# A two-layer attention megakernel: sums and deviations spread by way of DRAM, projection by adding transfers, the first image's keys first

## The chip, the cores and the metric

The kernel runs on one core of a Trainium2 chip. The metric is the device time of one execution in microseconds (us). Before the change it is 3413.48 us, the median of three runs between 3412.46 and 3414.23.

## The reference

The input is eight images of 256 channels and 32 × 32 positions, in fp32. Two layers follow each other.

```python
# layer 0, per image: group norm, then attention over a pooled pyramid
q  = einsum('bchw,oc->bohw', x, q_w)            # 1024 queries, 8 heads of 32
kv = einsum('bchw,oc->bohw', x, kv_w)
# k and v maps: pooled to 32x32, 16x16, 11x11, 5x5 -> 1426 tokens;
# each level p becomes p + depthwise3x3(p) + bias; then layer norm over channels
attn = softmax(q_g @ k.T * 32**-0.5); out_att = attn @ v
# a small channel attention of the heads (w_attn) and the projection follow
x = x + proj(...)

# layer 1, per image: 1024 tokens of 256 channels
t = t + attn1(layernorm(t))      # one head of 256
t = t + moe(layernorm(t))        # 8 experts of three 256x256 layers, softmax gates
```

The gates of the experts depend on the mean over all eight images, so that they are known only when layer 1's attention of the last image has ended.

## The kernel before, in words

Everything lies as channels on the 128 partitions (two halves, `c` or `k`) by positions in the free dimension. All work in fp32.

**The spine.** `attention` (line 880) runs 384 steps in order: 8 images × 2 halves of the channels (4 heads each) × 2 halves of the queries × 12 chunks of 128 keys. A step makes scores (`scores`, line 1458: four matmuls of 32 rows into the `sc` bank), one exponential of 128 × 2048 on ScalarE into one of six `pt` buffers (line 1465), and, a step later, the product with the values (`values`, line 1468). Every second step an adding transfer from the POOL queue adds one `pt` to the one before it (`add`, line 1480). After 12 steps the unit's sum of exponentials is formed: VectorE adds the pairs (line 1494), four matmuls add over the partitions (line 1499), so that each of the four heads' 512 sums stands 32 times, once on each of its partitions, in `rec` (128 × 512). `normalise` (line 1506) takes the reciprocal of all 128 × 512 and multiplies the unit's output `att` by it. ScalarE adds up sums and reciprocals for a check of their bounds. There are 32 such units.

**The background.** All other work of layers 0 and 1 lies in Python generators ("threads"), which yield what they need next (an engine and tiles). The class `Flow` (line 656) keeps a model of each engine's time while the program is being written, with a cost for every instruction (`cost`, line 711) and a lag until its result is there. For a transfer the lag is 3.0 us from the SP queue and `LANDING` = 9.5 us from POOL (line 784). After each step `Flow.step` (line 849) lets those threads go on whose inputs are, by this model, near enough; `NEAR` and `AHEAD` (lines 35 and 36) say how near for each engine. `finish` (line 862) drives threads until a condition holds. The order on every engine is fixed by this, and on the chip each engine, and each engine's transfer queue, goes through it in order.

**The first image.** Nothing can hide its preparation: `prepare` (line 1337) normalises the image, `first_maps` (line 1128) makes its key and value maps, values first (m = 2, 3) and keys (m = 0, 1) after, and then the queries. The large level's 3 × 3 taps of the keys run on TensorE as diagonal matmuls (`first_keys`, line 1179, with diagonals from `first_diagonals`, line 1116), those of the values and all small levels on VectorE (`first_taps`, line 1217). `by_tokens` (line 1254) turns them into normalised tokens. The spine starts when two of three groups of keys are there (line 1803). The diagonals (line 1119), the second value map's `p` (line 1136), and the two key maps' `p` and `acc` (lines 1139 and 1141) lie in buffers of the `pt` ring until used. For later images the taps all run on VectorE (`convolve`, line 1229).

**The projection.** When an image's four units are done, `project` (line 1514) makes four matmul pairs of 128 × 512. For each it loads a quarter of the image's x into the only `xr` buffer (line 1525), VectorE adds product, bias and x there (line 1533), and the sum is stored to `t1` in DRAM (line 1535). The last image goes through one big buffer.

**Layer 1.** `layer1` (line 1577) loads `t1`, and `scale_tokens` (line 1540) divides each token by its deviation: transposes to tokens (line 1550), statistics on VectorE, a power on POOL, and then the row of 128 × tiles deviations must be spread over all partitions. For that POOL multiplies the identity by the deviations (`diag`, line 1560), and a matmul with ones puts them on every partition (line 1568); VectorE multiplies by what stands in PSUM (line 1573). This happens once per image for 1024 tokens (two pieces of 512) and once for each 256 tokens of layer 1's output (`norm`, line 1679).

**The experts** (`experts`, line 1979) take over TensorE when the spine has ended, while the last image's layer 1 still runs in the background. Until the gates are known, `first` (line 2117) makes an expert's first layer as 8 products of 256 columns; later, `first7` (line 2213) makes it as 7.

Of the kernel before, what the change touches and what calls it, by code (L numbers as in the profile page):

```python
# [11 lines left out]
ALU = mybir.AluOpType  # L12
# [4 lines left out]
P = 128  # L17
# [18 lines left out]
NEAR = {"DVE": 1.5, "ACT": 2.0, "POOL": 1.0, "SP": 10.0}  # L36
BUFS = {"sm": 2, "sx": 1}
PACE2 = 8.0
LANDING = 9.5
# [616 lines left out]
class Flow:  # L656
# [90 lines left out]
    def note(self, engine, op, ins, args, kwargs):  # L747
# [35 lines left out]
        if "dma" in op:  # L783
            lag = 3.0 if engine == "SP" else LANDING
# [95 lines left out]
def attention(tc, kit, f, outer, ended, nb, consts, x, t1, t2, hn, bounds, vecs, q_t, kv_t, proj_t, gqk_t, wqk, wqkv, vecs1, w1_d, w1c, gate_d, wrc, vecs2, bnvec):  # L880
# [6 lines left out]
    with ExitStack() as ctx:  # L887
# [38 lines left out]
        pjw = weight(proj_t, "v", 256, l1)  # L926
# [27 lines left out]
        def mix():  # L954
# [66 lines left out]
            bdt = T(l1, [P, 2, P], "diag4")  # L1021
# [40 lines left out]
        def pool(*tiles):  # L1062
            return "POOL", tiles, None

# [49 lines left out]
        first, large, whole, pooled = {}, [], [], []  # L1114

        def first_diagonals():

            middle = T(l1, [P, 2, P], "rec1")
            rest = T(work, [P, 4, 512], "pt", bufs=6).rearrange("p a (b q) -> p (a b) q", q=P)
# [8 lines left out]
        def first_maps(xp):  # L1128


            for m in (2, 3, 0, 1):
                c = m % 2
                if m == 2:
                    p, acc = pmap, T(work, [P, NK], "acc", bufs=3)
                elif m == 3:
                    p = T(work, [P, 4, 512], "pt", bufs=6).rearrange("p j q -> p (j q)")
                    acc = T(work, [P, NK], "acc", bufs=3)
                else:
                    both = T(work, [P, 4, 512], "pt", bufs=6).rearrange("p j q -> p (j q)")
                    p = both  # L1140
                    acc = T(work, [P, 4, 512], "pt", bufs=6).rearrange("p j q -> p (j q)")
                for t in (p, acc):
                    if t is not pmap:
                        f.split(t, 512, HW)
                first[m] = p, acc
            for s0, w in KEY_SLICES:
                if s0 >= HW:
                    yield until(lambda: pooled)
                for m in (2, 3, 0, 1):
                    c = m % 2  # L1150
                    p, acc = first[m]
                    src = source(xp, s0, w)
                    yield pe(src, tag="sm")
                    ps = small()
                    for k in range(2):
                        f.pe.matmul(
                            ps[:, :w],
                            lhsT=kvw[:, k, m * P : (m + 1) * P],
                            rhs=src[:, k, :],
                            start=k == 0,  # L1160
                            stop=k == 1,
                        )
                    f.act.activation(p[:, s0 : s0 + w], ps[:, :w], AF.Copy)
                    for s, n in enumerate(SIDES):
                        a, z = max(OFFS[s], s0), min(OFFS[s] + n * n, s0 + w)
                        if a < z and (m >= 2 or s):
                            f.act.activation(
                                acc[:, a:z],
                                ps[:, a - s0 : z - s0],
                                AF.Identity,  # L1170
                                bias=db(c, s),
                                scale=mid[:, c * 4 + s : c * 4 + s + 1],
                            )
                if s0 == 512:
                    large.append("maps")
                    f.spawn(first_keys(), 5)
            whole.append("maps")

        def first_keys():
# [3 lines left out]
            for half in range(2):  # L1183
                for m in range(2):
                    p, acc = first[m]
                    pin = p[:, : n * n].rearrange("p (h w) -> p h w", h=n)
                    yield pe(p[:, : n * n], middle, rest, tag="sm")
                    ps = small()
                    pout = ps.rearrange("p (h w) -> p h w", w=n)
                    for i, tap in enumerate((4, 0, 1, 2, 3, 5, 6, 7, 8)):  # L1190
                        dy, dx, y0, y1, x0, x1 = windows(tap, n)
                        y0, y1 = max(y0, 16 * half), min(y1, 16 * half + 16)
                        f.pe.matmul(
                            pout[:, y0 - 16 * half : y1 - 16 * half, x0:x1],
                            lhsT=rest[:, 8 * m + i - 1, :] if i else middle[:, m, :],
                            rhs=pin[:, y0 + dy : y1 + dy, x0 + dx : x1 + dx],
                            start=i == 0,
                            stop=i == 8,
                        )
                    f.act.activation(acc[:, half * 512 : half * 512 + 512], ps, AF.Identity, bias=db(m, 0))  # L1200
                large.append(("keys", half))
# [135 lines left out]
        def prepare(b):  # L1337

            xi = xs.pop(b) if b in xs else load_x(b)
# [1125 lines left out]
```

## Time and profile before

| | us | share of the span |
|---|---|---|
| span of the profiled execution | 3418.4 | |
| TensorE matmul busy (PE) | 3204.7 | 94% |
| TensorE weight load busy (PEld) | 1781.8 | 52% |
| VectorE busy (DVE) | 2285.8 | 67% |
| ScalarE busy (ACT) | 1675.6 | 49% |
| GpSimd busy (POOL) | 499.0 | 15% |

A row of the groups says: line, engine, operation, output <- inputs, shapes, count, busy time and mean in nanoseconds, and then the idle time before these instructions with what ended it. All recorded operations go through one helper, so that all carry line 669; the tiles' names tell them apart. An fp32 matmul of the program is two records in the profile. A row of the waits says who waited for whom: us in total, times, the longest. In the table of transfers the numbers are KB of each and us from issue to landing.

### The profile page before, as it was taken

What the parts mean: (1) busy time and instruction counts of PE and PEld (TensorE: products, weight loads), DVE (VectorE), ACT (ScalarE), POOL (GpSimd) and SP (SyncE); (2) the same over time, 40 slices, a digit from 0 to 9 for tenths busy, and PEclk for the clock granted to TensorE, in tenths of its full rate; (3) what the DMA queues carried; (4) which work ended last, traced back from release to release, by engine and by line L of the source; (5) the groups of instructions that cost most, each with busy time, mean ns of one, the idle gap of its engine ahead of it and who ended that gap; (6) DMA issues with size and microseconds to landing.
All of it is one profiled execution on the core that took longest, in us unless ns stands there. A gap on an engine that the chain in (4) does not pass through costs nothing.

```text
span 3418.4 us, 39922 instructions
## 1 busy us (share of the span) xinstructions
PE 3204.7 (94%) x15264; PEld 1781.8 (52%) x15264; DVE 2285.8 (67%) x3914; ACT 1675.6 (49%) x2193; POOL 499.0 (15%) x616
## 2 busy tenths in 40 slices
PE   7588899999999899999999989998999999999998
PEld 3232244444444334434434356646777777777776
DVE  6587798888888878888644543216776666666665
ACT  3466667566676576566664523342223333333332
POOL 3122213122141221321211200004000000000000
PEclk9699999999999999999999999999999999999999
DMA  1257565555555655555665663123440000000000
GB/s 48 63 114 165 135 135 115 125 126 123 138 116 122 161 108 128 127 122 129 148 134 132 141 191 124 56 77 132 140 160 31 19 29 27 19 19 19 19 13 20
DMA packets 105032, 337.47 MB, mean 99 GB/s; under 512 B 12976, under 2 KB 38328, under 8 KB 81600
## 3 DMA queue, kind: packets, MB, share of 16 engines
q0 software_dynamic: 24576, 172.51, 25.8%
q1 hardware_dynamic: 76896, 160.35, 13.6%
q8 instruction: 122, 2.00, 0.2%
q10 hardware_dynamic: 3360, 1.97, 0.2%
q14 instruction: 78, 0.64, 0.1%
HBM read 98.33 MB, written 63.97 MB: 47 GB/s over the span
## 4 chain that ended last, share of the span: by engine, by line
PE 74%; DMA 5%; ACT 4%; DVE 2%; issue 2%; POOL 1%; SPq 0%; ACTq 0%; DVEq 0%; POOLq 0%
PE bank L669 25%; PE sm L669 18%; PE y L669 11%; PE sc L669 8%; PE sx L669 6%; PE pv L669 6%; ACT pt L669 3%; DMA pt<-pt 2%; DMA t<-xr 1%; DMA xr<-in_x_dram 1%; DVE acc L669 0%; DMA hn<-hn 0%; DVE pt L669 0%; DVE rec L669 0%; DVE xr L669 0%
## 5 line engine op out<-in xcount | busy, mean ns | idle before, releaser
L669 ACT ACTIVATE pt<-sc 128x2048 f32<-128x2048 f32 (+1 forms) x384 | 720.7, 1877 | 317.1 <-PE sc L669 244.7
L669 PE MATMUL sc<-q,kn 32*128 32x512 f32 (+1 forms) x3072 | 452.4, 659 | 115.5 <-ACT pt L669 114.0
L669 DVE SCALAR_TENSOR_TENSOR acc<-p,vec,acc 128x225 f32<-128x225 f32 (+7 forms) x928 | 528.5, 576 | 35.7 <-ACT acc L669 11.2
L669 PE MATMUL bank<-h,w2e 128*128 128x512 f32 x1024 | 480.5, 595 | 0.0
L669 ACT ACTIVATE h<-bank,bnvec 128x512 f32<-128x512 f32 x302 | 233.1, 772 | 484.5 <-PE bank L669 464.4
L669 DVE TENSOR_TENSOR pt<-pt,pt 128x1024 f32<-128x1024 f32 x320 | 390.0, 1261 | 84.8 <-DMA pt<-pt 82.6
L669 PE MATMUL pv<-pt,vt 128*32 128x512 f32 (+1 forms) x3072 | 422.6, 623 | 0.0
L669 ACT ACTIVATE h<-c,bnvec 128x512 f32<-128x512 f32 x210 | 159.6, 807 | 318.6 <-DVE c L669 318.6
L669 POOL DMA_DIRECT2D pt<-pt x192 | 169.8, 884 | 923.2 <-ACT pt L669 788.8
L669 DVE TENSOR_TENSOR c<-p1c,bank 128x512 f32<-128x512 f32 x105 | 72.2, 688 | 314.9 <-PE bank L669 314.9
L669 PEld LDWEIGHTS sc<-q,kn 32*128 32x128 f32 (+1 forms) x3072 | 117.8, 181 | 311.5 <-ACT pt L669 209.4
L669 PEld LDWEIGHTS bank<-h,w2e 128*128 128x128 f32 x1024 | 194.8, 191 | 153.0 <-issue 141.4
L669 PEld LDWEIGHTS pv<-pt,vt 128*32 128x32 f32 (+1 forms) x3072 | 61.0, 109 | 306.6 <-issue 291.4
L669 POOL TENSOR_TENSOR rstd<-rstd,mhalf 128x4 f32<-128x4 f32 (+2 forms) x88 | 107.0, 1216 | 733.8 <-DVE rstd L669 593.7
L669 DVE TENSOR_TENSOR h<-h,gates 128x1024 f32<-128x1024 f32 x128 | 156.9, 1226 | 71.3 <-DMA h<-h 64.2
L669 PE MATMUL bank<-hn,w1e 128*128 128x256 f32 (+1 forms) x604 | 192.7, 448 | 10.1 <-DMA hn<-hn 10.1
L669 PE MATMUL y<-t,s3e 128*128 128x256 f32 x768 | 187.1, 380 | 0.0
L669 PE MATMUL sm<-p,v 128*128 128x256 f32 x736 | 173.8, 388 | 6.1 <-DVE xr L669 6.1
L669 ACT ACTIVATE p<-sm 128x512 f32<-128x512 f32 (+1 forms) x154 | 89.9, 584 | 173.7 <-PE sm L669 134.2
L669 PE MATMUL sm<-y,t 128*128 128x256 f32 x712 | 169.4, 385 | 2.1 <-ACT p L669 2.1
L669 PEld LDWEIGHTS bank<-hn,w1e 128*128 128x128 f32 x604 | 114.7, 191 | 99.9 <-issue 92.4
L669 PEld LDWEIGHTS sm<-p,v 128*128 128x128 f32 x736 | 139.3, 193 | 49.7 <-issue 24.4
(294 smaller groups left out, 4624.9 us busy)
## 6 DMA issues: line engine op xcount, KB each, us to landing
pt<-pt POOLq DMA_DIRECT2D x160, 1024.0 KB, 7.3
h<-h SPq DMA_DIRECT2D x80, 512.0 KB, 3.4
xi<-in_x_dram SPq DMA_DIRECT2D x16, 512.0 KB, 5.0
t<-t SPq DMA_DIRECT2D x8, 1024.0 KB, 6.9
res<-t SPq DMA_DIRECT2D x32, 256.0 KB, 4.4
t<-res SPq DMA_DIRECT2D x32, 256.0 KB, 2.6
hn<-res SPq DMA_DIRECT2D x32, 256.0 KB, 3.4
hn<-hn SPq DMA_DIRECT2D x16, 512.0 KB, 5.8
```

The lines of the kernel that those rows point to most:

```text
L669: ins = fn(*args, **kwargs)
```

## The change

It has four parts.

- **Reciprocals once each.** The 4 × 512 different sums of a unit are regathered by a transfer from `rec` into a 128 × 16 tile `few`, VectorE takes the reciprocal of those, they are stored as a 4 × 512 row in DRAM, and four transfers spread each head's row over its 32 partitions of `rec`. The check's sum is taken over `few`.
- **Layer 1's deviations by the same way.** In `scale_tokens` the deviations go to a row in DRAM and come back on all partitions, in place of diagonals on POOL, matmuls with ones, and a PSUM bank. So that the store is contiguous, a transpose now takes every eighth (or second) token.
- **Projection by adding transfers.** x is copied into `t1` from DRAM to DRAM when the image is prepared. ScalarE adds the bias and writes the product to `xr`, and a POOL-queue transfer adds it onto `t1`. The last image is left as it was.
- **First image's keys first.** The large level's keys are mapped first, its queries are a thread of their own, the spine starts with one group of keys, and the buffers are placed elsewhere: diagonals in layer 1's `t`, key accumulators in `kn` and `v`, the second value map in `acc`; only the key maps' `p` stay in the `pt` ring. In turn the fifth step must wait for all taps of the keys.

The model of the transfers is made finer (a lag that grows with the size), and SP transfers are issued only when their input is within 1 us of being there.

```diff
-NEAR = {"DVE": 1.5, "ACT": 2.0, "POOL": 1.0, "SP": 10.0}
+NEAR = {"DVE": 1.5, "ACT": 2.0, "POOL": 1.0, "SP": 1.0}
...
-            lag = 3.0 if engine == "SP" else LANDING
+            size = 4e-3 * out.shape[0] * out.free_size() if out.space != DRAM else 4e-3 * srcs[0].shape[0] * srcs[0].free_size()
+            lag = 2.0 + 0.0045 * size if engine == "SP" else 1.5 + 0.0078 * size
...
-            rest = T(work, [P, 4, 512], "pt", bufs=6).rearrange("p a (b q) -> p (a b) q", q=P)
+            rest = T(l1, [P, 16, P], "t")
...
-            for m in (2, 3, 0, 1):
...
+            for m in range(4):
+                if m < 2:
                     p = T(work, [P, 4, 512], "pt", bufs=6).rearrange("p j q -> p (j q)")
+                    acc = T(l1, [P, NK], "v") if m else T(work, [P, NK], "kn", bufs=3)
+                else:
+                    p = T(work, [P, NK], "acc", bufs=3) if m == 3 else pmap
                     acc = T(work, [P, NK], "acc", bufs=3)
...
+            for m, s0 in [(m, s0) for g in (0, 2) for s0 in (0, 512) for m in (g, g + 1)] + [(m, HW) for m in range(4)]:
...
+                    f.spawn(first_keys(0), 1)
+                    f.spawn(first_keys(1), 5)
...
+            if b < nb - 1:
+                f.sp.dma_start(t1[b], x[b].rearrange("(k p) n -> p k n", p=P))
...
+                f.spawn(queries(b, xi), 3)
                 yield from first_maps(xp)
...
-            return rec
+            few = T(work, [P, 16], "few")
+            yield sp(rec)
+            f.sp.dma_start(few, rec[::DH, :].rearrange("j (i k) -> j i k", k=16))
+            return rec, few
...
-            f.ve.reciprocal(rec, rec)
+            yield ve(few)
+            f.ve.reciprocal(few, few)
+            yield sp(few)
+            f.sp.dma_start(rows[n].rearrange("j (i k) -> (j i) k", k=16), few)
+            yield sp(rows[n])
+            for j in range(4):
+                f.sp.dma_start(rec[DH * j : DH * j + DH, :], rows[n][j : j + 1, :].to_broadcast([DH, 512]))
+            yield act(few)
+            f.act.activation(few, few, AF.Copy, accum_out=lo[:, column[n] : column[n] + 1])
+            yield ve(rec)
             f.ve.tensor_tensor(att, att, rec, ALU.mult)
...
-                        xt = T(work, [P, 512], "xr")
-                        f.sp.dma_start(xt, x[b, m * P : (m + 1) * P, sl])
...
+                        yield act(ps)
+                        f.act.activation(xt, ps, AF.Identity, bias=bias[:, m : m + 1])
+                        yield pool(xt)
+                        f.pool.dma_start(out=t1[b][:, m, sl], in_=xt, accum_op=ALU.add)
...
-                        f.pe.transpose(ps[:, o : o + P], src[:, c, (g + u) * P : (g + u + 1) * P], ident)
+                        f.pe.transpose(ps[:, o : o + P], src[:, c, g + u :: tiles], ident)
...
-                diag = T(l1, [P, m, P], f"diag{m}")
...
-                    rb[:, : m * P], lhsT=kit.ones, rhs=diag.rearrange("p t q -> p (t q)"), start=True, stop=True
...
+            f.sp.dma_start(row.rearrange("o (p u) -> (o p) u", u=tiles), r)
+            yield sp(row)
+            w = min(512, n)
+            for o in range(0, n, w):
+                rb = T(l1, [P, w], f"rb{w}")
+                f.sp.dma_start(rb, row[:, o : o + w].to_broadcast([P, w]))
                 yield ve(rb)
-                f.ve.tensor_tensor(d, d, rb[:, None, : m * P].to_broadcast([P, 2, m * P]), ALU.mult)
+                f.ve.tensor_tensor(d, d, rb[:, None, :].to_broadcast([P, 2, w]), ALU.mult)
...
-        f.finish(lambda: key_parts[0] > 1)
+        f.finish(lambda: key_parts[0] > 0)
...
+                if i == 4:
+                    f.finish(lambda: {0, 1}.issubset(whole))
```

## The prediction

> **What bounds the kernel now.** I read the page from the top: spans first, then busy time by engine, then the slices.
>
> ```profile
> span 3418.4 us, 39922 instructions
> PE 3204.7 (94%) x15264; PEld 1781.8 (52%) x15264; DVE 2285.8 (67%) x3914; ACT 1675.6 (49%) x2193; POOL 499.0 (15%) x616
> ...
> PE   7588899999999899999999989998999999999998
> ...
> DVE  6587798888888878888644543216776666666665
> ...
> PEclk9699999999999999999999999999999999999999
> ```
>
> TensorE is busy 94% of the span and idle 213 us. So time leaves in two ways: less TensorE work, or fewer of these 213 us. The low digits stand in the first slices. The table of stretches puts numbers on them (columns: length, then busy time of PE, PEld, DVE, ACT, POOL, then granted clock, DMA share, GB/s):
>
> ```profile
> 0.00:102.00 102.00, 68.56 (x191) 34.88 (x192) 70.33 (x161) 39.10 (x82) 35.43 (x57) 0.91 0.13 40
> 102.00:190.00 88.00, 62.46 (x319) 27.60 (x317) 46.09 (x121) 42.07 (x50) 10.51 (x9) 0.78 0.34 73
> 190.00:500.00 310.00, 262.49 (x1526) 94.80 (x1523) 256.91 (x448) 207.91 (x239) 67.20 (x78) 0.95 0.63 138
> 500.00:2000.00 1500.00, 1429.80 (x8119) 659.62 (x8118) 1132.10 (x1953) 928.95 (x1107) 332.38 (x389) 0.98 0.58 129
> ...
> 2350.00:3418.00 1068.00, 1054.39 (x4052) 769.42 (x4050) 675.27 (x1050) 345.56 (x539) 7.29 (x14) 0.99 0.14 47
> ```
>
> TensorE idles 33 us before 102 us, 26 to 190, 48 to 500, then 70 in 1500 us, and 14 in the last 1068. In the last stretch the experts run at TensorE's pace, and the change doesn't touch them. What TensorE waits for between 110 and 2030 us, from the waits:
>
> ```profile
> PE sc L669 <- ACT pt L669: 114.0, 95, 7.1
> PE sm L669 <- DVE xr L669: 12.3, 3, 6.1
> PE bank L669 <- DMA hn<-hn: 10.1, 1, 10.1
> ```
>
> The scores wait for the exponential ahead to empty their bank. Why that is late at the start, the timeline shows:
>
> ```profile
> 89.15 1.95 PE L669 MATMUL sx<-con,kt 128*128 128x128 f32 x4 [12.54 <-ACT kt L669]
> ...
> 102.46 2.09 PE L669 MATMUL sc<-q,kn 32*128 32x512 f32 x8
> ...
> 128.35 1.88 ACT L669 ACTIVATE pt<-sc 128x2048 f32<-128x2048 f32 x1 [6.43 <-DMA pt<-pt]
> ...
> 143.87 1.88 ACT L669 ACTIVATE pt<-sc 128x2048 f32<-128x2048 f32 x1 [7.98 <-DMA pt<-pt]
> ```
>
> The first score starts at 102.46, after TensorE idled for the first keys. Then the exponentials wait for adding transfers: by lines 1119 to 1141 the first image's diagonals and maps hold all six `pt` buffers, so each step lives on one just freed.
>
> **What the Trainium skill says.** "TensorE: Matmul & The Clock Gate", Part 1, states that an idle array is clocked at half rate until busy again. The trace agrees: granted 0.78 at 102 to 190 us, against 0.98 later, so idle time there costs twice. "DMA: Bandwidth & Descriptors", Anatomy of one DMA, prices a transfer at about 2 us whatever its size; the smallest ones here took 3.1 to 3.9 us, which I use. "SBUF — State Buffer", SBUF: two separate sides, states that a GpSimd-issued transfer can stall behind a VectorE instruction holding the shared port; the waits show POOL pt behind DVE acc for 42.5 us in six cases. The same title, Door 1, says that reads stepping over 16-byte lines pay a penalty; no transpose before does this, so no run shows it.
>
> **The change, part by part.** The rows used, from the groups kept apart by shape and the table of transfers:
>
> ```profile
> L669 DVE RECIPROCAL rec<-rec 128x512 f32<-128x512 f32 x32 | 107.2, 3352 | 64.6 <-ACT rec L669 64.6
> L669 DVE SCALAR_TENSOR_TENSOR xr<-sm,mtb,xr 128x512 f32<-128x512 f32 x19 | 14.2, 748 | 30.6 <-DMA xr<-in_x_dram 22.9 <-PE sm L669 5.6 <-issue 2.1
> L669 PE MATMUL sm<-diag,con 128*128 128x256 f32 x48 | 15.4, 403 | 0.0
> ```
>
> ```profile
> pt<-pt POOLq DMA_DIRECT2D x160, 1024.0 KB, 7.3
> t<-xr SPq DMA_DIRECT2D x28, 256.0 KB, 3.0
> wr<-in_gate_dram SPq DMA_DIRECT2D x1, 8.0 KB, 3.1
> ```
>
> 1. *Deviations by way of DRAM.* The 48 spreading matmuls go: 16 of 512 columns and 32 of 256. A matmul is two records; a record of 512 columns follows its predecessor after 0.43 us (four take 1.72 us, 46.13 to 47.85), one of 256 after half. So 16 × 0.86 + 32 × 0.43 = 27.5 us of TensorE. POOL loses 45 us of diagonals, on no path. TensorE has 95% to do from 500 us on, so I count -24. The changed order has 41 plain first expert layers before the gates are known, against 38: 8 products of 256 columns instead of 7, so 3 × 0.43 = +1.3. The transposes now load every eighth (128 of them) or every second (128) column. If a load of 0.14 us took double, the eight-step ones would cost 128 × 0.14 = 18 us; if they hide under the matmul ahead, none. I take 3.
>
> 2. *Reciprocals once each.* VectorE loses 32 × 3.35 = 107 us and gains 32 small reciprocals at no more than 0.2 each, 6 us. In exchange the sums go through three transfers (regather, store, load four times), each started when the one before has landed. At 3 us each that is 9 us against 3.4, some 6 later per unit. Queued behind the multiplication on VectorE are the next taps. In the changed order 9 to 15 us of other VectorE work mostly lies between small reciprocal and multiplication, as little as 1 to 5 in six of 32 units, so mostly nothing waits. Behind a waiting transfer on the SP queue are loads of x, queries and residuals; they are early enough.
>
> 3. *Projection by adding transfers.* VectorE loses 28 × 0.75 = 21 us, ScalarE gains 28 × 0.6 = 17 (its copy of `rec` was 0.63 × 32, now 512 times less wide, which pays for it). The 28 loads of x and their waits go: that is the 12.3 us of TensorE behind `xr`. A 256 KB add joins the POOL queue's 192. Its landing lies between 3.0 (the plain store) and 3.0 + 7.3, behind a full-size add; a late landing holds the one `xr` buffer and so ScalarE. I keep 8 of the 12.3. The copy of x into `t1`, 1 MB per image, runs far ahead: nothing.
>
> 4. *First keys first.* In the changed order, TensorE has before its first score 12 map and query groups of 4 records (20.6 us), four convolutions of 18 records (31), four groups of pooled levels (5.4) and 32 transposes (4.8). From 14.35 us on that is 76; with 3 us of waits 79, so 23 earlier. Further, diagonals and maps now hold two `pt` buffers, not six: the 19 us that TensorE waits for those exponentials at 114 to 146 us should halve, -10. VectorE limits both: scores of step 5 wait for all the first image's taps, 16 × 1.24 + 4 × 8.5 = 54 us, plus statistics, from some 34 us on, about 100 to 112. The fifth exponential ran at 128. I take -32 for the start.
>
> 5. *VectorE relief* after 500 us: 122 of about 1640 us. The 50 us of TensorE waiting for exponentials there come partly from it (`pt` buffers freed by its sums): -10.
>
> 6. *New waits.* 80 chains (32 units, 48 norms) at a miss of 0 to 4 us on VectorE are 0 to 320 us of its idle, which it has; on TensorE I take +10, and at the end, where the last image's chain is bare, +3 more.
>
> Sum: -24 + 1 + 3 - 8 - 32 - 10 + 13 = -57, and with the better clock in the start (26 us of idle at 0.78; some 4 us) -61. 3413.5 - 61 = 3352.
>
> **The rivals.** (a) *Only the matmuls count*: image 1's taps fill VectorE (257 of 310 us at 190 to 500), so the start's gain is given back by the second image. For it: that very row. Against: `pt` waits, not VectorE, held steps 3 to 7. Then -24 to -27: about 3387. (b) *The waits move*: regathering, storing and spreading come late on VectorE in order; half of 320 us less the 122 saved, and a stalled exponential behind `xr` 28 times 4 us. About +40 beyond everything gained by parts 1 and 4: 3450. For it: the scheduler assumes 2 us and something for small transfers, and 3.1 was measured. Against: the distances in part 2, and that TensorE waits for transfers three times only between 110 and 2030 us, 13 us in all. (c) *Relief goes deeper*: the start gains 50, waits after 500 us fall by 30 and `xr` goes wholly: -27 - 50 - 30 - 12 = -119, about 3295.
>
> **How the numbers follow.** Forecast 0.55; (a) 0.23; (b) 0.10; (c) 0.12. The range takes in (a) and ends short of (c) by 10: 3305 to 3400. Beyond it lie (b) and most of (c). Faster by over 0.2%: 0.89; within: 0.02; slower 0.09.
>
> **What would show it.** Right: no `diag` matmul rows; TensorE busy some 25 us lower; first score near 79; no exponential waiting over 5 us for `pt<-pt` before 150; no TensorE wait for `xr`. Wrong: VectorE waiting for `rec<-row` or `rb` by tens of us, weight loads from `t` at twice 0.14 us, or ScalarE waiting on `xr` for `t<-xr`. If score steps of image 1 begin no earlier than now (340 us), (a) holds.

## The result and the profile after

The changed kernel takes 3473.12 us (median; 3472.83 to 3473.78), the kernel before 3413.79: a ratio of 1.0175 [1.0157, 1.0192]. It is slower by 59 us. The forecast was 3352 with a range of 3305 to 3400; the side on which it came out is that of rival (b), the waits move.

The head of the page after, to be held against the one of before (PEclk is the granted clock, the share of TensorE's full clock that the profile shows):

```profile
span 3470.9 us, 40221 instructions
...
PE 3207.0 (92%) x15168; PEld 1779.3 (51%) x15168; DVE 2150.4 (62%) x3886; ACT 1679.7 (48%) x2221; POOL 485.2 (14%) x596
...
PE   8687798899999999899899897998999999999998
...
PEclk9799999999999999999999998999999999999999
```

96 matmul records are gone (48 matmuls) and 135 us of VectorE, as meant. But TensorE's busy time has not fallen (3204.7 to 3207.0), and its idle time has grown from 213.7 to 263.9 us. The table by stretches, with the same columns as before, shows where:

```profile
0.00:102.00 102.00, 79.79 (x266) 38.56 (x266) 65.52 (x148) 49.35 (x90) 34.00 (x57) 0.96 0.26 79
102.00:190.00 88.00, 62.38 (x286) 32.69 (x290) 57.12 (x145) 35.79 (x47) 12.73 (x12) 0.79 0.37 83
190.00:500.00 310.00, 252.14 (x1468) 86.59 (x1460) 215.59 (x417) 200.25 (x235) 66.94 (x78) 0.93 0.63 133
500.00:2000.00 1500.00, 1395.52 (x7826) 645.86 (x7818) 1014.33 (x1923) 910.16 (x1110) 317.66 (x371) 0.97 0.62 133
...
2350.00:3470.00 1120.00, 1094.20 (x4163) 791.04 (x4162) 695.87 (x1075) 360.48 (x561) 38.95 (x64) 0.99 0.15 50
```

Before 102 us TensorE idles 22 us instead of 33: the first image's part works. From 102 to 190 nothing is won (26 idle in both). From 190 to 500 it idles 58 instead of 48, from 500 to 2000 104 instead of 70. Exponentials start as follows, after against before: the first 22.7 us earlier, the thirteenth 2.8 earlier, that of step 192 3.4 later, 264 18.8 later, 324 52.3 later, the last (383) 67.9 later; what lies behind it gives 15 back, as less of TensorE's work is left there (1373.3 us against 1404.7). So the loss arises in the steady part, above all in its last third.

Who waits there? The waits of TensorE (from 110 to 2120 us, as the steady part ends later than before), VectorE and ScalarE after (us in total, times, longest):

```profile
PE sc L668 <- ACT pt L668: 130.7, 98, 5.6
```

```profile
DVE res L668 <- DMA rb<-dev: 123.3, 27, 11.1
DVE pt L668 <- DMA pt<-pt: 116.1, 43, 11.2
DVE few L668 <- DMA few<-rec: 106.4, 24, 10.0
...
DVE t L668 <- DMA rb<-in: 35.2, 11, 8.2
```

```profile
ACT p L668 <- DVE acc L668: 79.2, 22, 5.5
...
ACT few L668 <- DMA row<-few: 38.4, 12, 10.8
...
ACT xr L668 <- DMA t<-xr: 7.3, 3, 4.6
```

TensorE's wait for the exponential has gone from 114.0 to 130.7 us. VectorE now waits 265 us for the new transfers: 106 for the regathered sums and 158 for the spread deviations. ScalarE's wait for the taps (`p <- acc`: a key map is written into the buffer that the taps before it still read) has doubled from 39.2. And there is a new one on ScalarE that the prediction did not have at all, `few <- row<-few`: its bound check copies `few` onto itself, and must let the store finish reading it first.

How such a wait travels is seen at one place. Timeline of the kernel after (start, duration, engine, operation; in brackets the idle time before it and what ended it):

```profile
1697.81 2.35 DVE L668 TENSOR_TENSOR pt<-pt,pt 128x1024 f32<-128x1024 f32 x2
1698.31 0.33 SPq L668 DMA_DIRECT2D rb<-dev  x1
1699.45 1.14 PE L668 MATMUL sc<-q,kn 32*128 32x512 f32 x8 [1.05 <-ACT pt L668]
...
1702.95 0.69 DVE L668 TENSOR_TENSOR res<-res,rb 128x512 f32<-128x512 f32 x1 [2.79 <-DMA rb<-dev]
...
1705.04 2.15 DVE L668 SCALAR_TENSOR_TENSOR acc<-p,vec,acc 128x16 f32<-128x16 f32 x8
...
1707.29 0.51 ACT L668 ACTIVATE p<-sm 128x402 f32<-128x402 f32 x1 [4.75 <-DVE acc L668]
...
1709.30 1.85 ACT L668 ACTIVATE pt<-sc 18x2048 f32<-18x2048 f32 x1
...
1711.21 1.29 PE L668 MATMUL sc<-q,kn 32*128 32x512 f32 x8 [4.38 <-ACT pt L668]
```

VectorE has nothing to do from 1700.2 to 1702.95 but stands before the multiplication by `rb`, whose transfer was issued at 1698.31. Behind it in the same order are eight taps; ScalarE waits for these to release the map's buffer; the exponential is behind that; TensorE waits for the exponential. 2.79 us of VectorE's wait stand at the head of 4.38 us of TensorE's.

### The profile page after: what moved, and what is told of

The parts are those of the page before. It is cut to its first block, busy times and chain, and to the rows that moved or that the text cites. A ratio compares the mean times of both kernels' runs of the same rounds, so it can differ in the third digit from the quotient of the medians.

```text
span 3470.9 us, 40221 instructions
## 1 busy us (share of the span) xinstructions
PE 3207.0 (92%) x15168; PEld 1779.3 (51%) x15168; DVE 2150.4 (62%) x3886; ACT 1679.7 (48%) x2221; POOL 485.2 (14%) x596
## 4 chain that ended last, share of the span: by engine, by line
PE 45%; DMA 3%; DVE 1%; ACT 1%; issue 0%; SPq 0%; POOL 0%; ACTq 0%; DVEq 0%; POOLq 0%
PE bank L668 24%; PE y L668 11%; PE sm L668 6%; PE sx L668 2%; PE sc L668 2%; PE pv L668 2%; DMA dev<-rstd 1%; DMA hn<-hn 1%; ACT pt L668 1%; DMA rb<-dev 1%; DMA rb<-in 0%; DVE pt L668 0%; DMA w1e<-w1c 0%; DMA few<-rec 0%; DVE t L668 0%
## 5 line engine op out<-in xcount | busy, mean ns | idle before, releaser
L668 DVE SCALAR_TENSOR_TENSOR acc<-p,vec,acc 128x225 f32<-128x225 f32 (+7 forms) x928 | 517.3, 564 | 32.2 <-ACT acc L668 7.1
L668 DVE TENSOR_TENSOR pt<-pt,pt 128x1024 f32<-128x1024 f32 x320 | 380.3, 1233 | 123.4 <-DMA pt<-pt 116.1
```

The costliest lines, as they stand in the source:

```text
L668: ins = fn(*args, **kwargs)
```

## The experiments

Several theories stood. W: the new in-order waits on VectorE cost the time (and TensorE's relief is real). P: the planner's assumed delay of 2 us for a small transfer is too small, so that it places the consumers too near. O: the order of work as such is worse, whatever the transfers do. Further letters are explained where an expectation first uses them. The first four runs undo one part each, with the planner free to reorder; none of their results is where W had put it.

**Undo the reciprocals** (as in the kernel before: reciprocal of all 128 × 512):

```diff
-            f.sp.dma_start(few, rec[::DH, :].rearrange("j (i k) -> j i k", k=16))
...
-            f.ve.reciprocal(few, few)
...
+            f.ve.reciprocal(rec, rec)
             f.ve.tensor_tensor(att, att, rec, ALU.mult)
```

> The changed kernel with the reciprocals as before (all 128x512 of a unit on VectorE, no regathering, no row in DRAM); everything else stays changed. Theory W (VectorE, in order, waits for the new small transfers): VectorE waited 106 us for few<-rec and saves 101 us of reciprocals, so its net is near nothing: 3473 within 12. Theory S (the many small transfers in one SP queue hold one another up): with 192 of 243 new transfers gone, the deviations' waits (159 us in the changed kernel) fall by half and the time by 25 or more. Theory X (ScalarE is held by the single xr buffer): no change, within 5.

Measured: 3428.5 us, 1.0043 [1.0026, 1.0060]. The part costs 45 us in these surroundings, although it takes 105 us from VectorE. The waits for the deviations fall from 158 to 132 us, and not by half as S would have it.

**Undo the deviations** (diagonals and matmuls with ones again):

```diff
-            f.sp.dma_start(row.rearrange("o (p u) -> (o p) u", u=tiles), r)
...
-                f.sp.dma_start(rb, row[:, o : o + w].to_broadcast([P, w]))
+                f.pe.matmul(
+                    rb[:, : m * P], lhsT=kit.ones, rhs=diag.rearrange("p t q -> p (t q)"), start=True, stop=True
+                )
```

> The changed kernel with layer 1's deviations spread as before (diagonals on POOL, matmuls with ones, contiguous transposes); everything else stays changed. Theory W: VectorE loses 159 us of waits for rb, TensorE gets 27.5 us of matmuls back: about 3473 - 50 + 25 = 3448 or less. If only TensorE's work counted: 3473 + 27 = 3500. Theory X: 3500 as well.

Measured: 3471.6, 1.0172 [1.0154, 1.0189], 1.5 us under the changed kernel. TensorE is busy 18.4 us longer (3225.4), and the waits for the regathered sums grow from 106 to 170 us: in a new order, one wait gone made another longer.

**Undo the projection** (x loaded into `xr`, VectorE adds):

```diff
-                        f.act.activation(xt, ps, AF.Identity, bias=bias[:, m : m + 1])
-                        yield pool(xt)
-                        f.pool.dma_start(out=t1[b][:, m, sl], in_=xt, accum_op=ALU.add)
+                    f.ve.scalar_tensor_tensor(xt, ps, bias[:, m : m + 1], xt, ALU.add, ALU.add)
+                    if b < nb - 1:
+                        f.sp.dma_start(t1[b][:, m, sl], xt)
```

> The changed kernel with the projection as before (x loaded into xr, bias and x added on VectorE, plain store; no copy of x to t1, no adding transfers onto it). Theory X: the exponentials no longer wait behind xr and POOL's queue has 28 fewer adds: 30 us or more faster, 3440. Theory W: VectorE gets 21 us of work and 31 us of waits for x back: 3473 to 3490.

Measured: 3465.0, 1.0147 [1.0125, 1.0168]: the part costs 8 us here, far from X's 30.

**Undo the first image's part** (values first, buffers in the `pt` ring):

```diff
-            for m in range(4):
+            for m in (2, 3, 0, 1):
...
-        f.finish(lambda: key_parts[0] > 0)
+        f.finish(lambda: key_parts[0] > 1)
```

> The changed kernel with the first image prepared as before (values first, two groups of keys before the first step, diagonals and maps in the pt ring). By the change's trace the first step came 23 us earlier and the fifth 18 us later, and step 12 only 3 earlier. Theory W: the part is worth nothing by then, 3473 within 12. Rival F (the first image's waits displace layer work that is missing later): 15 us or more faster.

Measured: 3497.6, 1.0256 [1.0226, 1.0286]: the part is worth 24 us, the only one of the four that gains.

**The order alone.** Three kernels built on the one before: with the changed planner only, with the first image's part only, and with both.

```diff
-NEAR = {"DVE": 1.5, "ACT": 2.0, "POOL": 1.0, "SP": 10.0}
+NEAR = {"DVE": 1.5, "ACT": 2.0, "POOL": 1.0, "SP": 1.0}
...
-            lag = 3.0 if engine == "SP" else LANDING
+            lag = 2.0 + 0.0045 * size if engine == "SP" else 1.5 + 0.0078 * size
```

> The kernel before, with the changed planner alone (SP transfers issued within 1 us of their input, lags that grow with size). No operation changes. Theory P says the planner matters where it is wrong about waits; here its lags are nearer to the measured ones for large and small: within 12 us of before, either way. Rival N (holding SP transfers back until 1 us before costs by itself): 20 us or more slower than before.

> The kernel before with the first image's part alone (keys first, buffers moved, one group of keys before the first step) and the planner as before. Undoing this part in the changed kernel cost 24 us, so if the parts add up it gives 24: 3390. If the fifth step's wait eats it: 3410 to 3420.

> The first image's part and the changed planner, without the two DRAM ways and the adding transfers. If the parts add up: the first image's 24 us and what the planner alone does. With a planner that is neutral: 3390.

Measured: 3430.9 (1.0048 [1.0031, 1.0065]), 3433.9 (1.0056 [1.0039, 1.0073]) and 3401.7 (0.9961 [0.9949, 0.9972]). The first of these differs from the kernel before in its order only (two of the experts' first layers change from 7 products to 8 with it, 2 × 0.43 us by the prediction's price), and it is 19 us slower. The last exponential starts at 1976.8 us against 1976.7; what the new order adds lies behind it, where 15 us more of TensorE's work is left (1420.2 us against 1404.7). The first image's part is worth +22 us with the old planner and -29 with the new. So a new order moves this kernel by 20 to 30 us either way. A difference of that size between kernels whose order differs says little of the part that was edited, the four undoings included, and the following three keep the order of every engine as it is in the changed kernel.

**Same order, waits gone.** The small reciprocals read a constant tile instead of `few`, so that nothing on VectorE waits for the regathering; what is then spread are the sums, scaled down, and not their reciprocals:

```diff
-            f.ve.reciprocal(few, few)
+            f.note("DVE", "reciprocal", nc.vector.reciprocal(few1, few1), (few, few), {})
```

> The changed kernel with the order of every engine kept instruction by instruction, and only what the 32 small reciprocals read changed: a constant tile, so that VectorE never waits for few<-rec. All transfers still go. What is spread are the sums, scaled by 5e-7 on ScalarE, and not their reciprocals. Theory W (VectorE's standing in its queue costs the time): 106 us of waits go, a third to a half of them reaches the end: 3473 - 35 to - 53 = 3420 to 3438. Theory L (chain length) or S (the SP queue): the chain is as long as before and SP carries the same, 3473 within 8. Rival O (the order alone is bad): 3473 within 8.

The multiplication by the deviations reads ones instead of `rb`:

```diff
-                f.ve.tensor_tensor(d, d, rb[:, None, :].to_broadcast([P, 2, w]), ALU.mult)
+                ones = kit.ones[:, None, 0:1].to_broadcast([P, 2, w])
+                f.note("DVE", "tensor_tensor", nc.vector.tensor_tensor(d, d, ones, ALU.mult), (d, d, rb[:, None, :].to_broadcast([P, 2, w])), {})
```

> The changed kernel in the same order, where layer 1's 48 multiplications by deviations read a constant one and not rb, so that VectorE never waits for the deviations' transfers; layer 1 is left unnormalised. Theory W: 158 us of waits go, later and where VectorE has more room, so a fifth to a third: 3420 to 3441. Theories L, S, O: within 8 of 3473.

And both edits together:

> Both: the order kept, the small reciprocals and the deviations' multiplications read constants; reciprocals and layer 1's normalisation are left out. Theory W: the two add up or nearly: 3473 - 70 to - 100, which is at or below what is measured for the first image's part with the changed planner (3402): 3375 to 3405. Theory O: no gain, and then the order itself must be the cause.

Measured: 3448.9 (1.0103 [1.0087, 1.0120]), 3417.4 (1.0010 [1.0001, 1.0019]) and 3393.3 (0.9941 [0.9918, 0.9963]). The waits for the sums cost 24.2 us, those for the deviations 55.7, together 79.9, which is what taking both away gives (79.9; the fit is closer than the scatter, as the runs of the last kernel alone lie between 3386.6 and 3401.3). All transfers are still issued and all instructions are still in their places. This shows the cause of the loss: 265 us of waiting on VectorE become 80 at the end, three tenths. The last exponential starts at 1971.6 us instead of 2044.6, so that nearly all of it is won in the steady part. The place of the timeline above, in the kernel without both waits:

```profile
1643.73 0.33 SPq L668 DMA_DIRECT2D rb<-dev  x1
...
1645.38 0.69 DVE L1588 TENSOR_TENSOR res<-res,con 128x512 f32<-128x512 f32 x1
...
1647.47 2.15 DVE L668 SCALAR_TENSOR_TENSOR acc<-p,vec,acc 128x16 f32<-128x16 f32 x8
1649.72 0.51 ACT L668 ACTIVATE p<-sm 128x402 f32<-128x402 f32 x1 [0.64 <-PE sm L668]
...
1654.41 1.14 PE L668 MATMUL sc<-q,kn 32*128 32x512 f32 x8 [1.04 <-ACT pt L668]
```

The multiplication follows its predecessor, the taps are done in time, ScalarE waits 0.64 us for its matmul and not 4.75 for the taps, and the scores wait 1.04 us instead of 4.38. And the page:

```profile
PE 3176.2 (94%) x15168; PEld 1768.6 (52%) x15168; DVE 2150.4 (63%) x3887; ACT 1679.5 (50%) x2221; POOL 485.9 (14%) x596
```

The same 15168 records of TensorE are 30.8 us shorter, at a granted clock of 0.977 instead of 0.969 (busy time times clock is nearly equal, 3103 and 3108 us), and its idle time is 49.0 us shorter. So a third of the 80 us or somewhat more is not waiting but a slower clock that comes with it.

**Is it the planner's number?** A delay of 5 us instead of 2 for transfers of at most 128 KB from the SP queue; then 6 us for those of the two chains alone:

```diff
-            lag = 2.0 + 0.0045 * size if engine == "SP" else 1.5 + 0.0078 * size
+            lag = (5.0 if size <= 128 else 2.0) + 0.0045 * size if engine == "SP" else 1.5 + 0.0078 * size
```

> The changed kernel, with one number of its planner changed: transfers of up to 128 KB from the SP queue are planned with a lag of 5.0 us in place of 2.0 (the trace of the changed kernel showed 3 to 5 us per hop between issues and uses). The same work, the same transfers, another order. Theory P (the planner puts the waiting VectorE instructions too early, and VectorE then stands in its queue): waits of VectorE for few<-rec and rb fall from 265 us to under 120 and the time by 25 us or more, to 3448 or less. Theory L (the long chain itself, 19 us per unit, delays the projection and layer 1): no gain, 3473 to 3485, since the chain gets no shorter.

```diff
-            lag = 2.0 + 0.0045 * size if engine == "SP" else 1.5 + 0.0078 * size
+            lag = (6.0 if self.key(out).split("_")[0] in ("few", "row", "rec", "dev", "in", "rb") else 2.0) + 0.0045 * size if engine == "SP" else 1.5 + 0.0078 * size
```

> The whole changed kernel, planned with a lag of 6.0 us for each transfer of the two new chains and nothing else (all operations and results as in the changed kernel). Theory P: waits for few<-rec and rb fall under 100 us, time 3425 to 3445, at or below the 3444.5 of the coarser 5 us lag. Against P: over 3455.

Measured: 3444.5 (1.0081 [1.0064, 1.0099]) and 3480.7 (1.0202 [1.0185, 1.0219]). Waits of VectorE in the second:

```profile
DVE pt L668 <- DMA pt<-pt: 230.0, 68, 25.0
...
DVE res L668 <- DMA rb<-dev: 68.1, 11, 32.0
...
DVE few L668 <- DMA few<-rec: 55.3, 11, 9.5
...
DVE t L668 <- DMA rb<-in: 28.1, 9, 9.1
```

In the first the waits for the chains fall from 265 to 126 us and the time by 28.6, about as P expected. In the second they fall to 152 us, but the time doesn't follow, against P: sums of `pt` wait twice as long as in the changed kernel, and ScalarE waits 40.4 us on `xr` for its adding transfer (7.3). From copying the sums to the multiplication a unit now takes 40 us on average, against 18.7. "The planner's number is all of it" falls for the whole kernel: 3444.5 is still 32 us over the kernel before, and a larger number for the chains alone moves the waiting elsewhere.

**The parts alone, on a common base.** The base has the first image's part, the planner and the projection, and neither way by DRAM:

> First image's part, changed planner and the projection by adding transfers, without the two DRAM ways. The same without the projection part gave 3401.7. Undoing the projection in the changed kernel gave 8 us. Theory X (adding transfers hold ScalarE or POOL's queue): 3410 or more. If the loads of x were the dearer thing (44 us of VectorE waiting for them in that run): 3395 or less.

Measured: 3385.7, 0.9914 [0.9897, 0.9931]: 16 us under the same kernel without the projection's part (3401.7), in which that part therefore seems to gain. Then the base with the deviations by DRAM, but multiplied by ones (no wait), and with true deviations and the planner's 6 us for their transfers:

> First image, planner, projection and the deviations' way by DRAM, reciprocals as before, and the multiplications by deviations read a constant, so that VectorE doesn't wait; same order as the run without the reciprocals' part (3428.5). Layer 1 is left unnormalised. Theory W with the saving real: 3385.7 (no DRAM way at all) less 27 = 3359. If the removed matmuls don't reach the end: 3380 to 3390. If the order is bad beyond waits: over 3395.

> The same planner on the changed kernel with reciprocals as before: a version meant to be fast. Theory P with the matmuls' saving real: VectorE's waits for rb fall from 132 to under 50 us, 3428.5 less some 35 = 3385 to 3400, and if all is hidden 3360 to 3380. If the deviations' way can't win: over 3400, behind 3385.7.

Measured: 3393.6 (0.9947 [0.9930, 0.9965]) and 3386.2 (0.9921 [0.9904, 0.9937]). The second is a whole kernel, and with the base the fastest of all: both beat the kernel before by 28 us. The first is neither down to the 3359 of a real saving nor quite in the range for none. Against the 3428.5 of the first experiment, which differs from it in the planner's number only, it gains 42 us: without the reciprocals' chain the larger delay helps, though 83 us of waits are left and not under 50. Waits of VectorE in it, and its head:

```profile
DVE res L668 <- DMA rb<-dev: 65.4, 13, 15.9
...
DVE t L668 <- DMA rb<-in: 17.9, 6, 5.6
```

```profile
span 3382.5 us, 39757 instructions
...
PE 3178.5 (94%) x15156; PEld 1770.2 (52%) x15156; DVE 2249.6 (67%) x3875; ACT 1696.1 (50%) x2219; POOL 481.8 (14%) x596
```

The head of the base:

```profile
span 3388.2 us, 39921 instructions
...
PE 3206.2 (95%) x15270; PEld 1783.8 (53%) x15270; DVE 2267.8 (67%) x3890; ACT 1695.1 (50%) x2222; POOL 519.1 (15%) x644
```

TensorE is busy 27.7 us less at the same clock (0.977), and the medians differ by 0.4 us: its idle time is 204.0 instead of 182.0 us. Where the saving went, the exponentials show (durations, then the first and the last start), in the base and in this kernel:

```profile
L668 ACT ACTIVATE pt<-sc x384: 1850/1877/1943, 81.7 to 1974.3; 128x2048 f32<-128x2048 f32 x192
```

```profile
L668 ACT ACTIVATE pt<-sc x384: 1850/1877/1957, 82.1 to 1952.0; 128x2048 f32<-128x2048 f32 x192
```

The last one starts 22.3 us earlier, but what lies behind it takes 16.6 us longer, as the planner has left 15.0 us more of TensorE's work for it (1392.2 us against 1377.2). Between the first and the last, TensorE idles 151 us instead of 131. The 83 us of waits for `rb` could be the reason: at the rate of the first experiment's order, where 132 us of such waits cost 34.9 (3428.5 against 3393.6), they make some 22, an estimate. But the kernel with ones has no such waits and idles 155 us there, though in the first experiment's order and not in the base's. What the removed matmuls are worth where neither waits nor order take it back, no run shows.

**The reciprocals alone**, on the base, with a constant for `few` as above, so that VectorE doesn't wait for the regathering:

> First image, planner, projection and the reciprocals' way by DRAM, deviations as before, and the small reciprocals read a constant; same order as the run without the deviations' part (3471.6). The sums, scaled, are spread and not their reciprocals. Theory W: 170 us of waits go, 3471.6 - 60 to - 85 = 3387 to 3412. If VectorE's relief of 100 us is worth anything: under 3386. If the long chain or the SP queue costs by itself: over 3412.

Measured: 3423.2, 1.0023 [1.0013, 1.0033]. Against the 3471.6 of the same order with its 170 us of waits for the sums, 48 us are won; with the pair of the deviations (34.9 for 132) that is the cause once more, in two other orders. But it is still 37 us dearer than the base, more than W's 3412. Its waits of ScalarE:

```profile
ACT few L668 <- DMA row<-few: 50.5, 18, 6.2
ACT p L668 <- DVE acc L668: 47.3, 18, 5.5
```

Two more kernels in its order take away what is left of waiting for the chain: first ScalarE's, by copying `few` into a tile of its own, then VectorE's for `rec`, by multiplying with a constant.

```diff
-            f.act.activation(few, few, AF.Copy, accum_out=lo[:, column[n] : column[n] + 1])
+            f.note("ACT", "activation", nc.scalar.activation(few2, few, AF.Copy, accum_out=low), (few, few, AF.Copy), {"accum_out": low})
```

> The kernel with the reciprocals' part alone beside planner, projection and first image, its small reciprocals reading a constant tile (3423.2), and now also ScalarE's bound check copying `few` into a tile of its own instead of in place, so that it no longer waits for the store row<-few (50.5 us in 18 waits there, ahead of exponentials in ScalarE's order). The order on every engine is the same. It leaves out what that kernel left out: the true reciprocals. The kernel without either DRAM way takes 3385.7, so 37 us are to be explained. Theory S (ScalarE's in-order wait for the store is that cost): about a third to a half of 50 us comes back, 3398 to 3408, and PE sc <- ACT pt falls from 103 toward 87 us. Theory O (the order of the work, not a wait): 3420 to 3425.

```diff
-            f.ve.tensor_tensor(att, att, rec, ALU.mult)
+            f.note("DVE", "tensor_tensor", nc.vector.tensor_tensor(att, att, mill.to_broadcast([P, 512]), ALU.mult), (att, att, rec, ALU.mult), {})
```

> The run before it, and the unit's multiplication takes a constant instead of `rec` (same order again; the output is not normalised by the sums), so that VectorE no longer waits for rec<-row (26.5 us in 8 waits). No engine then waits for any transfer of the reciprocals' chain, while all its transfers are still issued. Theory S: another 5 to 15 us, 3388 to 3400, near the 3385.7 of the kernel without the chain; what is left would be the queue and the order. Theory O: still 3415 to 3425. In between, about 3405 to 3412: both have a share.

Measured: 3400.9 (0.9959 [0.9949, 0.9969]) and 3398.6 (0.9949 [0.9933, 0.9966]). The bound check, 0.22 us long and off every path one would draw, cost 22.3 us because it was written in place. VectorE's waits for `rec`, 37.1 us in 11 cases in the first of the two, cost 2.3, within the scatter: not every wait costs. The last expectation's "no engine then waits" was not met. ScalarE's waits in that kernel:

```profile
ACT p L668 <- DVE acc L668: 44.6, 18, 5.5
...
ACT few L1534 <- DMA few<-rec: 19.8, 11, 4.7
```

The check, freed of the store, now waits for the regathering itself, which VectorE's constant no longer covers. It need not be what is left to the base, 12.9 us. The exponentials of this kernel:

```profile
L668 ACT ACTIVATE pt<-sc x384: 1848/1877/1922, 83.9 to 1957.2; 128x2048 f32<-128x2048 f32 x192
```

The last one starts 17.1 us before the base's; what lies behind it takes 26.9 us longer, 24.0 of them more work of TensorE (1401.2 us against 1377.2). So the remainder arises behind the steady part, by what the planner's order left for it, and so do 26 of the 35 us by which the profiled execution of the reciprocals alone was longer than the base's. What the 19.8 us of waits still cost was not tried.

## Why the prediction was wrong, point by point

The forecast was -61 us, the result +59, a miss of 120. The kernel without VectorE's new waits takes 3393.3, 20 us under the kernel before; by the prediction's own sum it should be some 13 us under the forecast. So about 67 us of the miss are the waits on VectorE. About 54 are gains that did not come, or that a wait of ScalarE's took back, which is still in that kernel (for the store, 41.4 us; see step 6).

**Step 6, new waits, is the step that failed.** The chains' waits on VectorE were put at 0 to 320 us "of its idle, which it has", and for TensorE and the end +13 was taken. The 265 us measured lie inside the bound. Wrong was that idle time of an engine at 62% can be spent freely. It is idle because its next input is not there yet; an instruction that waits for a transfer stands in front of everything later in its order, and at the place shown these were taps on which a map buffer, ScalarE and the exponentials hang. The part measured 80 us, not 13. A second wait, ScalarE's for the store, was not in the sum at all, and cost 22 us where it was measured, on the base; in the changed kernel itself (38.4 us of it) it was not tried.

**Step 2, reciprocals**, had the chain at 9 us; from the copy of the sums to the multiplication it took 18.7 on average (10.6 to 39.8). The "3.1 to 3.9 us" of the smallest transfers left out two rows of the same table, 8 KB at 5.9 us (`wr<-wrc`) and 4 KB at 5.4 (`br<-in_gate_dram`). At their best the hops were short: from the issue of the regathering to the reciprocal 1.84 us, from store to spread 1.45. The Trainium skill, "DMA: Bandwidth & Descriptors", Anatomy of one DMA, states about 2 us as the fixed part of a transfer issued by GpSimd, to which a part that grows with the bytes is added; these were issued from the SP queue, and the shortest lie a little below it. But the medians are 3.5 and 3.7 us, and the longest 12.8 and 17.3. In 24 of the 32 regatherings VectorE stood waiting; how much of a hop was the queue, the other transfers or a late consumer was not measured. "9 to 15 us of other VectorE work mostly lies between" was a count of instructions between reciprocal and multiplication; the dear wait was at the other end, ahead of the reciprocal, where the prediction had not counted.

The new small reciprocals (durations: least, median, most, ns) took 0.25 us and not at most 0.2; the adding transfers (KB, us to landing) are as assumed:

```profile
L668 DVE RECIPROCAL few<-few x32: 223/253/254, 203.0 to 2059.1; 128x16 f32<-128x16 f32 x32
```

```profile
t<-xr POOLq DMA_DIRECT2D x28, 256.0 KB, 4.5
```

**Step 1, deviations**, was right in the matmuls, 27.5 us forecast and 23.5 (without waits) and 27.7 (with the 6 us) measured on the base. The step from there to -24 at the end failed: as shown above, it became idle time in the steady part, and a longer stretch behind it. The +1.3 for three more plain first layers of the experts was nothing: both traces have 23 of them (184 records of 512 columns, eight to a layer). The strided transposes' weight loads grew from 141 ns (median, before) to 193 where every eighth column is loaded (`t`), and from 140 to 208 where every second is (`res`):

```profile
L668 PEld LDWEIGHTS sm<-con,t x84: 185/193/230, 420.7 to 2136.6; 128*128 128x128 f32 x84
```

```profile
L668 PEld LDWEIGHTS sm<-con,res x108: 194/208/230, 530.9 to 2272.1; 128*128 128x128 f32 x108
```

The Trainium skill ("SBUF — State Buffer", Door 1) states that each read that crosses to a new 16-byte line pays a penalty, and that steps of up to 4 fp32 elements are free. A penalty is there, of a third to a half and not of double. But the step of two elements, free by the page, pays more than the step of eight, so the page's rule does not describe these loads. The transposes themselves grew from 273 ns to 276 and 283; for 128 of each that is 1.7 us of TensorE, so the 3 us taken is not contradicted.

**Step 3, projection.** Right in its mechanism: no wait of TensorE for `xr` is left, the landing of 4.5 us lies in the forecast 3.0 to 10.3, and ScalarE's wait behind it is 7.3 us. The worth is not settled: +8 in the changed kernel, -16 beside the first image's part and the planner, -8 forecast, all within what order does. Two readings were off. `few` is 32 times less wide than `rec`, not 512; ScalarE is busy 4 us longer in sum. And the 42.5 us of POOL behind `acc` are no sign of a shared port: all six adding transfers start 0.3 to 0.5 us after the end of an exponential, so that they may simply have waited for what they add. No run here shows a transfer held up by the port.

**Step 4, first keys first,** was right in its first half. The first score starts at 80.03 (forecast 79). The second half was not. Exponentials of the kernel after:

```profile
83.30 1.88 ACT L668 ACTIVATE pt<-sc 128x2048 f32<-128x2048 f32 x1
...
146.39 1.88 ACT L668 ACTIVATE pt<-sc 128x2048 f32<-128x2048 f32 x1 [0.58 <-PE sc L668]
```

The fifth comes at 146.39, not about 100 to 112, and 18 us later than before. The step had the taps as what it waits for. On the chip it is TensorE's order:

```profile
97.66 0.60 PE L668 MATMUL sx<-con,kt 128*128 128x128 f32 x4
...
141.65 3.48 PE L668 MATMUL sx<-res,p 128*128 128x256 f32 x8 [4.66 <-DMA res<-in_w_dram]
145.06 1.26 PE L668 MATMUL sc<-q,kn 32*128 32x512 f32 x8
```

The second group of keys is transposed by 98.3, and taps of the second key map still run on VectorE from 141.62 to 150.14, beside the fifth scores. What stands ahead of these in TensorE's order is layer 1's weights, which the planner placed there while it finished the taps, and TensorE waits in them: 5.95 and 8.02 us for VectorE, whose own order has taps ahead of its share, and at the end 4.66 us for a weight to be loaded. By the thirteenth the start is ahead by 2.8 us only, and image 1 begins at 346.2 instead of 340.5: rival (a)'s mark. Undoing the part costs 24 us all the same, against 32 forecast; with the caution of the order again.

**Step 5, VectorE's relief** of 10 us: not seen. With the sums' and deviations' waits gone VectorE is busy 2150 us, 117 less than in the base, and the kernel is 8 us slower than the base. Its order is another, and ScalarE's wait for the store is in it, so that a relief could be hidden. (VectorE's busy time after 500 us was 1912 us, not about 1640.)

**The clock's -4** counted on less idle time between 102 and 190 us. There nothing changed (26 us idle, clock 0.78 and 0.79); over the whole span the clock fell from 0.974 to 0.969 as idle time grew. That idle time "costs twice" is more than the runs show: with the order held, 49.0 us more of it came with 30.8 us of longer matmuls.

**The rivals.** (b) had the right mechanism, and its 3450 is 23 us off. That is partly luck: its terms (160 less 122, and 28 × 4 = 112 for ScalarE behind `xr`) make 150, less the 56 of parts 1 and 4 some 94 and not 40; and `xr` measured 7.3 us, not 112. It was given 0.10 in part because the prediction counted TensorE's own waits for transfers before (three, 13 us) as evidence. They say nothing of waits that reach TensorE by way of two other engines. The marks set down for "wrong" were of use: VectorE waits 158 us for `rb`, though only 2.7 for `rec<-row`.

## What to carry to other kernels

Before work is taken from an engine at the price of a round trip, list for each new wait what stands behind it in that engine's order and who waits for that, on every engine that touches the new tiles, the small checks included; an in-order engine's idle time is not free. Here three tenths of the new waits came back at the end (23 to 35% in the pairs of equal order but one, where 2.3 of 37.1 us did): it depends on what stands behind. A small copy that is written in place over a transfer's source waits for that transfer: a tile of its own took it off. And where a planner fixes the order, first measure what a mere change of order does (here 20 to 30 us), see how much work it leaves for the end, and compare causes with the order held still.

## What the runs showed of the hardware

With the order held, more idle time of TensorE came with a lower granted clock. Idle 263.9, 249.7, 223.1 and 214.9 us (the changed kernel, without the waits for sums, for deviations, for both) went with 0.969, 0.971, 0.973 and 0.977; between the first and the last, the same matmul records took 30.8 us longer. In kernels of different order it need not: 182.0 and 204.0 us went with the same 0.977.

The 8 KB of regathered sums were used 1.84 us after the issue of their transfer at best, after 3.5 in the median and after 12.8 at most, in the steady part, where the DMA engines are busy 62% of the time; a unit's way of three transfers, planned with 2.0 to 2.3 us each, took 18.7 on average.

A weight load of 128 × 128 in fp32 took a median of 141 ns from adjacent columns, 193 from every eighth and 208 from every second.
